# The clip of the projected rows of batch 1 moves from VectorE on PSUM to GpSimd on SBUF

## The chip, the cores and the metric

The kernel runs on one core of a Trainium2 chip. The time is the device time of one execution in microseconds. Before the change the median of three runs is 1516.16 us (1514.95 to 1519.41).

A core has five engines that matter here, each with a queue of its own that it works through in order: TensorE (PE in the profile), VectorE (DVE), ScalarE (ACT), GpSimd (POOL) and SyncE (SP), which only issues DMAs. GpSimd issues DMAs from its queue too. Engines wait for each other by semaphores. Matmuls write to PSUM, which has eight banks; SBUF holds everything else that is on the chip.

## The reference, cut to what matters

One transformer block whose attention and linear layer work beside each other on the same normalised input; B = 2, S = 1024, D = 1024, 32 heads of 32 channels, all in float32.

```python
xn  = layernorm(x)
qkv = clip(xn @ Wqkv.T, -8, 8)              # clip on all of q, k and v
q, k, v = split(qkv)
q = layer_norm(q, q_ln_w, q_ln_b)           # over all 1024 channels
k = layer_norm(k, k_ln_w, k_ln_b)
scores = q @ k.T * 32**-0.5 + slope[h] * (kpos - qpos), causal
attn = softmax(scores) @ v @ Wout.T
out = x + attn + (xn @ binarized(weight).T + bias)
```

The clip at 8 stands between the projections and the normalisation of q and k, and ahead of the use of v.

## The kernel before

**Projections.** Tokens go in pairs of 128-token tiles; batch b has four pairs. For one pair and one of k, q, v, the product with a 1024x1024 weight is made as a 2x2 block product with seven products in place of eight (`seven`, line 622). Each of the seven takes four matmuls of 128x512 into one PSUM bank, in the order 11, 21, t2, t3, t4, t1, 22. `combine` (line 643) adds the products up: `take` (line 672) is called after each of the seven; product 11 goes to SBUF by ScalarE, t2, t3 and t1 become running sums `u` and `u3` in SBUF by one VectorE operation each (`plus`, `less`), and the four halves of the two finished rows come out in `whole` (line 664): row a gets its first half from product 21 and its second from 22, row b from t4 and t1. `whole` first adds the running sum to the bank in place, on VectorE, and then clips the bank into the row (`kraw`, `qraw` or `vraw`, 128x1024), again on VectorE. For the output projection `bound` is None, and one add writes the row.

**What follows a row.** When row b is whole (after t1) and when row a is (after 22), `ready` is called. For k and q, `to_channels` (line 835) is put among the side jobs: statistics of both halves on VectorE (`stats_of`, line 703; BATCH_NORM_STATS2 in the profile), their aggregate, the reciprocal root on ScalarE (`spread`, line 709), a few short VectorE operations, the normalisation in place on ScalarE, transposes in 32x32 blocks on VectorE, and DMAs to DRAM from GpSimd's queue. For v, GpSimd's queue issues the DMA of the row at once.

**Attention.** A block is one batch, 512 query rows and a group of four heads; there are 32. `first_scores` (line 1276) makes scores for a unit of rows in four banks and takes their maximum on VectorE (CUSTOM_DVE on `s`, with `rel`; the read of `mx` follows); after that these banks are free. `shifts` (line 1313) turns the maxima into bf16 rows: five short GpSimd operations on `sh` and `shift_b`, then, one step later, a transpose `trs` on TensorE. `second_scores` (line 1337) makes transposed scores in four banks, less the shift, adds the causal mask on VectorE (`behind`), and ScalarE's exponential writes `pT`. `add_up_parts` (line 1411) sums the `pT` tiles of a block on GpSimd; the sum is the denominator that `divide` (line 1446) reads with the matmuls `den`. `weigh_values` multiplies `pT` with the values.

**Order.** Nothing is rescheduled: each engine executes its instructions in the order in which the program issues them. Batch 0's projections stand first (0 to some 320 us). The loop over steps (line 1520) then issues, per step, one unit of first scores, the shifts of a closed block, the denominators, the weighing, one unit of second scores, and then `fill` (line 1166), which issues a share of the remaining products one after the other: batch 1's k, q and v projections during batch 0's attention, then the binary linear layer and the output projection during batch 1's. After each two products' pieces `fill` advances the side jobs. So a projection's VectorE and GpSimd operations stand between those of two steps of attention.

**Banks.** Seven of the eight PSUM banks are shared by scores and products. `score_bank` (line 565) picks, at build time, the bank that has been idle longest by a model of the engines' times (`Clocks`, line 83 for the durations of one instruction); the eighth holds the weighed values. A matmul into a bank waits until its last reader is done. A row tile (`raw_tile`, line 556) has four buffers.

All operations of the kernel are recorded by one helper, so their line in the profile is L148, and they are told apart by their tiles: `mm_k` and `mm_k_t` are the products of k (t for those with a summed weight), `kraw` its rows; likewise q and v.

Of the kernel before, what the change touches and what calls it, by code (L numbers as in the profile page):

```python
# [12 lines left out]
ALU = mybir.AluOpType  # L13
# [21 lines left out]
class Clocks:  # L35
# [35 lines left out]
    def ready(self, eng, outs, ins):  # L71
        t = 0.0
        for ap, also_read in [(a, False) for a in ins] + [(a, True) for a in outs]:
            name = ap.tensor.name
            t = max(t, self.free.get(name, 0.0))
            p0, p1, lo, hi = self.spot(ap)
            for (q0, q1, l, h), (w, r, by) in self.log.get(name, {}).items():
                w = 0.0 if by == eng == "pe" else w
                if q0 < p1 and p0 < q1 and l < hi and lo < h:
                    t = max(t, w, r if also_read else 0.0)  # L80
        return t
# [112 lines left out]
def parallel_block_kernel(  # L194
# [37 lines left out]
    nc = Program(tc.nc, clocks)  # L232
# [170 lines left out]
    def half(n):  # L403
        return slice(n * HALF, (n + 1) * HALF)
# [154 lines left out]
    def half_tile(name):  # L559
        return work.tile([P, HALF], FP, tag="half", name=name, bufs=2)  # L560
# [82 lines left out]
    def combine(name, ra, rb, ready, rest=None, bound=None):  # L643


        h = {}

        def put(i, n):
            if rest:
                row = (ra, rb)[i][:, half(n)]  # L650
                if (i, n) != (0, 1):
                    nc.gpsimd.tensor_tensor(row, row, rest[i][:, half(n)], ALU.add)
                ready(i, row, n)

        def plus(dst, ps, other, op=ALU.add):
            nc.vector.tensor_tensor(dst, ps, other, op)

        def less(dst, ps, other):
            plus(dst, ps, other, ALU.subtract)

        def whole(i, n, ps, other, op=ALU.add):
            row = (ra, rb)[i][:, half(n)]
            if bound is None:
                plus(row, ps, other, op)
            else:
                plus(ps, ps, other, op)
                nc.vector.tensor_scalar(row, ps, -bound, bound, ALU.max, ALU.min)  # L670

        def take(block, ps):
            if block == "11":
                h["u"] = half_tile(f"u_{name}")
                nc.scalar.copy(h["u"], ps)
            elif block == "21":
                whole(0, 0, ps, h["u"])
                put(0, 0)
            elif block == "t2":
                plus(h["u"], ps, h["u"])  # L680
            elif block == "t3":
                h["u3"] = half_tile(f"u3_{name}")
                plus(h["u3"], ps, h["u"])
            elif block == "t4":
                whole(1, 0, ps, h["u3"])
                put(1, 0)
            elif block == "t1":
                less(h["u"], ps, h["u"])
                whole(1, 1, ps, h.pop("u3"), ALU.subtract)
                put(1, 1)  # L690
                if rest:
                    nc.gpsimd.tensor_tensor(h["u"], h["u"], rest[0][:, half(1)], ALU.add)
                else:
                    ready(1, rb)
            else:
                whole(0, 1, ps, h.pop("u"))
                put(0, 1)
                if not rest:
                    ready(0, ra)

        return take
# [719 lines left out]
    late = []  # L1421
# [187 lines left out]
```

## Time and profile before

| | |
|---|---|
| median of three runs | 1516.16 us (1514.95 to 1519.41) |
| profiled execution's own time | 1518.33 us |
| its span | 1516.5 us |
| mean granted TensorE clock | 0.994 |
| TensorE busy | 1473.9 us (97%) |
| VectorE busy | 967.2 us (64%) |
| GpSimd busy | 1045.4 us (69%) |
| ScalarE busy | 630.1 us (42%) |
| clip of a half row, VectorE, 128x512 | 0.692 us, 96 of them |
| add in place in a bank, VectorE, 128x512 | 0.695 us for mm_k |
| statistics of a half row, VectorE | 0.680 us |
| two-input add, GpSimd, 128x512 | 1.311 us |

How to read the profile's rows: times are microseconds, unless they are in a mean per instruction, which is in nanoseconds. A group's row gives engine, operation, written tile, an arrow and the tiles read, the shape and count, then busy time and mean, then the idle time just before these instructions and what ended it. A row of waits gives who waited, for whom, the sum, how many times, and the longest. A row of stretches gives the stretch and its length, then busy time and count of instructions of PE, PEld (weight loads), DVE, ACT and POOL, the granted clock, and the share and rate of the DMA engines. A row of the timeline gives the start, the duration from the first to the last of like instructions, the instruction, how many, and in brackets how long the engine had been idle and what ended that.

### The profile page before, as it was taken

How to read it: one execution, taken by the hardware profiler on the slowest of the kernel's cores; microseconds unless marked ns; L12 is line 12 of the kernel's file. 1: busy time of each engine (PE TensorE's matmuls, PEld its weight loads, DVE VectorE, ACT ScalarE, POOL GpSimd, SP SyncE). 2: the span in 40 equal slices, each digit the busy share in tenths (PEclk: the TensorE clock that was granted, in tenths of full speed). 3: DMA queues.
4: the chain of work that ended last, by engine and by line, in shares of the span. 5: the costliest groups of instructions: out<-in, count | busy, mean ns of one | idle time of the engine just before them, and what ended most of it. 6: DMA issues, size and time to landing. Idle time of an engine off the chain costs nothing.

```text
span 1516.5 us, 24240 instructions
## 1 busy us (share of the span) xinstructions
PE 1473.9 (97%) x8060; PEld 637.5 (42%) x8060; DVE 967.2 (64%) x2718; ACT 630.1 (42%) x1203; POOL 1045.4 (69%) x1336
## 2 busy tenths in 40 slices
PE   7999999999999999999999999999999999999998
PEld 3444444444434333333333344555655333333333
DVE  6866586868778776677556565666655666555322
ACT  3322132204556543544343573655554444443430
POOL 4587287333886678768747698767788778777661
PEclk9999999999999999999999998999999999999999
DMA  8889389682436764699335476667678213321232
GB/s 298 277 271 303 100 271 283 221 296 77 137 102 206 235 188 87 158 224 299 98 121 174 155 242 160 152 135 162 146 159 230 61 52 97 91 65 42 60 80 56
DMA packets 140909, 249.08 MB, mean 164 GB/s; under 512 B 12528, under 2 KB 69360, under 8 KB 138992
## 3 DMA queue, kind: packets, MB, share of 16 engines
q1 hardware_dynamic: 111392, 153.14, 31.1%
q0 software_dynamic: 29392, 94.39, 25.9%
q8 instruction: 64, 1.05, 0.3%
q14 instruction: 61, 0.50, 0.1%
HBM read 159.66 MB, written 107.74 MB: 176 GB/s over the span
## 4 chain that ended last, share of the span: by engine, by line
PE 82%; DVE 10%; issue 3%; POOL 2%; DMA 1%; ACT 1%; POOLq 0%; DVEq 0%; ACTq 0%; SPq 0%
PE s L148 20%; PE mm_f L148 8%; PE mm_o_t L148 7%; PE o L148 7%; PE mm_v_t L148 7%; PE mm_q_t L148 7%; PE mm_k_t L148 6%; PE mm_o L148 5%; PE mm_v L148 5%; PE mm_q L148 5%; DVE s L148 3%; PE mm_k L148 3%; PE den L148 2%; DMA x<-in_x_dram 1%; DVE mx L148 1%
## 5 line engine op out<-in xcount | busy, mean ns | idle before, releaser
L148 POOL TENSOR_TENSOR pT<-pT,pT 128x512 f32<-128x512 f32 (+3 forms) x628 | 579.5, 980 | 129.5 <-ACT pT L148 119.1
L148 ACT ACTIVATE pT<-s,kpos 128x512 f32<-128x512 f32 (+3 forms) x768 | 378.2, 590 | 441.0 <-DVE s L148 271.2
L148 DVE CUSTOM_DVE_ANT_0 s<-s,rel 128x512 f32<-128x512 f32 (+3 forms) x512 | 283.4, 600 | 54.4 <-PE s L148 47.9
L148 PE MATMUL s<-kg,qg 32*128 32x512 f32 (+3 forms) x1536 | 169.7, 523 | 1.4 <-DVE qraw L148 0.9
L148 PE MATMUL s<-qg,kg 32*128 32x512 f32 (+3 forms) x1536 | 164.6, 500 | 0.0
L148 PE MATMUL o<-pT,vg 128*32 128x512 f32 (+3 forms) x1536 | 157.7, 495 | 2.5 <-ACT pT L148 2.5
L148 DVE CUSTOM_DVE_ANT_0 s<-s,rel,mx 128x512 f32<-128x512 f32 (+3 forms) x256 | 140.9, 589 | 23.8 <-PE s L148 21.5
L148 PE MATMUL mm_f<-sg,hl 128*128 128x512 f32 x512 | 126.2, 399 | 2.1 <-DVE mx L148 2.1
L148 PE MATMUL mm_o_t<-w_o_t,ot 128*128 128x512 f32 x256 | 116.5, 601 | 0.0
L148 DVE TENSOR_TENSOR s<-s,behind 128x256 f32<-128x256 f32 (+1 forms) x320 | 98.7, 378 | 24.6 <-PE s L148 24.6
L148 PEld LDWEIGHTS s<-kg,qg 32*128 32x128 f32 x1536 | 66.6, 184 | 109.5 <-issue 71.7
L148 DVE DVE_READ_ACCUMULATOR2_ANT mx<- 128x1 f32 x768 | 109.1, 142 | 0.0
L148 PEld LDWEIGHTS mm_f<-sg,hl 128*128 128x128 f32 x512 | 93.9, 188 | 33.4 <-DVE mx L148 12.5
L148 PE MATMUL mm_v_t<-w_v_t,xp 128*128 128x512 f32 x224 | 101.7, 600 | 2.0 <-POOL w_v_t L148 1.6
L148 PE MATMUL mm_q_t<-w_q_t,xp 128*128 128x512 f32 x224 | 100.6, 598 | 0.0
L148 PE MATMUL s<-rows,minus_b 12*128 12x512 bf16 (+3 forms) x768 | 82.7, 329 | 14.1 <-DVE mx L148 13.3
L148 PEld LDWEIGHTS s<-qg,kg 32*128 32x128 f32 x1536 | 77.2, 185 | 29.3 <-issue 20.4
L148 PE MATMUL mm_v<-w_v,xp 128*128 128x512 f32 x192 | 88.6, 609 | 0.0
L148 PE MATMUL mm_o<-w_o,ot 128*128 128x512 f32 x192 | 87.8, 602 | 0.0
L148 PE MATMUL mm_q<-w_q,xp 128*128 128x512 f32 x192 | 86.3, 598 | 0.0
L148 PEld LDWEIGHTS o<-pT,vg 128*32 128x32 f32 x1536 | 39.2, 109 | 109.3 <-issue 90.2
L148 POOL TENSOR_TENSOR ot<-inv,ot 128x512 f32<-128x512 f32 x16 | 20.4, 1272 | 85.4 <-ACT inv L148 85.4
(201 smaller groups left out, 1863.3 us busy)
## 6 DMA issues: line engine op xcount, KB each, us to landing
xp<-xd SPq DMA_DIRECT2D x8, 1792.0 KB, 8.2
kg<-kd SPq DMA_DIRECT2D x48, 256.0 KB, 5.2
vg<-vd SPq DMA_DIRECT2D x48, 256.0 KB, 5.9
wd_ot<-in_wout_t_dram POOLq DMA_DIRECT2D x11, 1024.0 KB, 9.5
x<-in_x_dram SPq DMA_DIRECT2D x16, 512.0 KB, 5.8
qg<-qd SPq DMA_DIRECT2D x32, 256.0 KB, 6.3
vd<-vraw POOLq DMA_DIRECT2D x16, 512.0 KB, 6.5
out_dram<-in_x_dram SPq DMA_DIRECT2D x16, 512.0 KB, 7.7
```

The source lines that it names most:

```text
L148: result = real(*args, **kw)
```

## The change

For batch 1 (the second character of the name is the batch: `k1_0` is pair 0 of k of batch 1), the last add of a half row writes the row in SBUF, unclipped, and reads the bank only once; GpSimd then clips the half row in place in SBUF. For batch 0 the two VectorE operations stay as they are: an add in place in the bank, and the clip from the bank into the row.

```diff
             row = (ra, rb)[i][:, half(n)]
             if bound is None:
                 plus(row, ps, other, op)
-            else:
-                plus(ps, ps, other, op)
-                nc.vector.tensor_scalar(row, ps, -bound, bound, ALU.max, ALU.min)
+                return
+            late = name[1] != "0"
+            plus(row if late else ps, ps, other, op)
+            eng, src = (nc.gpsimd, row) if late else (nc.vector, ps)
+            eng.tensor_scalar(row, src, -bound, bound, ALU.max, ALU.min)
```

In the built program the order of the instructions on every engine is the same but for this: 48 clips are missing from VectorE's queue, and 48 stand in GpSimd's, each where the half row came out. The model that picks the banks sees the changed operations, so some score tiles and products lie in another bank than before.

## The prediction

> **What bounds the kernel now.** I read the page first: shares of busy time, slices, and the chain that ended last.
>
> ```profile
> span 1516.5 us, 24240 instructions
> PE 1473.9 (97%) x8060; PEld 637.5 (42%) x8060; DVE 967.2 (64%) x2718; ACT 630.1 (42%) x1203; POOL 1045.4 (69%) x1336
> PE 82%; DVE 10%; issue 3%; POOL 2%; DMA 1%; ACT 1%; POOLq 0%; DVEq 0%; ACTq 0%; SPq 0%
> ```
>
> TensorE is busy 97% of the span and carries 82% of the chain. VectorE has a tenth of the chain although it is 64% busy. So a shorter VectorE pays only where TensorE waits for it. Batch 1's projections stand between 320 and 910 us (first and last kraw to vraw clip of that batch: 331 and 902 us), so I asked for the busy time of three stretches there and for TensorE's waits between 320 and 910 us.
>
> ```profile
> 320.00:520.00 200.00, 193.52 (x1255) 80.06 (x1255) 156.97 (x475) 96.82 (x200) 126.97 (x189) 1.00 0.53 160
> 520.00:720.00 200.00, 194.33 (x1087) 73.93 (x1086) 142.71 (x403) 91.51 (x173) 153.94 (x176) 0.99 0.71 187
> 720.00:910.00 190.00, 184.91 (x1074) 72.96 (x1073) 111.86 (x323) 95.63 (x176) 136.31 (x158) 1.00 0.49 159
> PE s L148 <- DVE mx L148: 11.7, 32, 0.9
> PE mm_k_t L148 <- DVE mx L148: 1.3, 3, 0.4
> PE den L148 <- DVE vraw L148: 1.1, 1, 1.1
> PE trs L148 <- POOL shift_b L148: 0.5, 1, 0.5
> ```
>
> The columns of the first three are PE, PEld, DVE, ACT, POOL. TensorE idles 590.0 - 572.8 = 17.2 us, nearly all of it waiting for VectorE to free a score bank: many short waits, the longest 1.1 us. That is the ceiling of any gain. GpSimd is already 64, 77 and 72% busy, and it runs in order.
>
> **Prices.** From the groups of VectorE and GpSimd, shapes kept apart, and from the tiles rel and kpos:
>
> ```profile
> L148 DVE TENSOR_SCALAR kraw<-mm_k 128x512 f32<-128x512 f32 x16 | 11.1, 692 | 0.5
> L148 DVE TENSOR_TENSOR or<-mm_o,u_o 128x512 f32<-128x512 f32 x16 | 11.1, 692 | 44.3 <-PE mm_o L148 29.3 <-issue 10.8 <-POOL u_o L148 2.6
> L148 POOL TENSOR_TENSOR pT<-pT,pT 128x512 f32<-128x512 f32 x256 | 320.0, 1311 | 72.8 <-ACT pT L148 72.6
> L148 POOL TENSOR_SCALAR_AFFINE_SELECT rel<-rel x1: 1041/1041/1041, 2.3 to 2.3; 128x1024 f32<-128x1024 f32 x1
> L148 POOL TENSOR_SCALAR kpos<-off x32: 220/233/692, 11.9 to 40.3; 128x8 f32<-128x8 f32 x32
> ```
>
> **Part 1, the clip leaves VectorE.** 48 clips (three projections, four pairs of token tiles, four quarters) of 0.69 us: 33.2 us off VectorE. The add that remains costs the same into SBUF as in place: 0.692 us for or<-mm_o,u_o, which already reads PSUM and writes SBUF, against 0.695 us for mm_k<-mm_k,u_k. In the timeline I went through TensorE's 46 waits between 320 and 910 us. 29 of them follow a clip within 6 us with VectorE idle at most 0.15 us in between, so the clip itself made the score bank late there. Each recovers at most its own length or the clip's 0.69 us; together 10.2 us. The other 7 us follow a stretch in which VectorE had itself waited for TensorE, and stay. Bounds of the gain: 0 (every wait is replaced by the next bank's) and 10.2 us; I take all of it less what part 3 spoils, since these waits are shorter than the clip.
>
> **Part 2, GpSimd gets 48 clips.** No row shows a 128x512 one-input operation with two ALU steps on GpSimd. The nearest rows: the affine select of 1024 elements (1.04 us), and kpos with 8 elements (0.233 us median). The slope of the affine select is (1041 - 293)/896 = 0.835 ns an element (the 128x128 one on ident took 293 ns), so 512 elements make 0.61 us by that row and 0.233 + 504 x 0.835 ns = 0.65 us by kpos with that slope. Upper end: the two-input add, 1.31 us. I take 0.65 us, as the same operation is nearest, and keep 0.61 to 1.31. Load: 48 x 0.65 = 31 us on 417 us busy in 590, so 76%; it does not become the bound by load. The Trainium skill ("GPSIMD Engine Reference", section Engine selection) speaks against the change: elementwise work belongs on VectorE, GpSimd being about twice as slow for two inputs and roughly at line rate for one. By twice VectorE's 0.69 us a clip would be 1.38 us and the sum below about +4.4 us instead of -1.7; the slope of the affine select stands on the side of the one-input half of that rule. No run here yet shows the clip itself.
>
> What is queued behind a clip on GpSimd: where the row is written after GpSimd had got there, it waits for VectorE's add, and the shift chain behind it (sh, shift_b, read by the transpose trs on TensorE) starts late. That happens at 327, 343 and 369 us, by 4.9, 4.2 and 5.1 us. But trs follows one step later, at 341.7, 360.2 and 384.4 us, against shift_b at 328.3, 344.7 and 370.7: 9 to 15 us of slack. Cost 0. At 897.3 us the slack is 1.9 us (shift_b ends 895.35); two clips ahead of it and TensorE's own gain of 0.9 us in that stretch leave -0.3: cost 0.4 us. The last sums that the denominators read end 2 us or more before the den matmuls; one clip fits. The value rows' DMAs are issued by GpSimd behind the clip anyway, up to 2.5 us later, and are loaded much later: 0. SP issues nothing different.
>
> **Part 3, a new wait.** After product t1 of a pair (row b) and after product 22 (row a) VectorE's next step for a q or k row is its statistics (BATCH_NORM_STATS2 on both halves). They used to follow VectorE's own clip. Now they wait for GpSimd, which must first finish the probability sums queued ahead, and behind them on VectorE stand the next add and the score maxima that free TensorE's banks. The worst place:
>
> ```profile
> 402.85 8.24 POOL L148 TENSOR_TENSOR pT<-pT,pT 128x384 f32<-128x384 f32 x12
> 405.20 0.69 DVE L148 TENSOR_TENSOR mm_k_t<-mm_k_t,u_k 128x512 f32<-128x512 f32 x1
> 406.53 1.28 DVE L148 BATCH_NORM_STATS2 stats_k<-kraw 128x6 f32<-128x512 f32 x2
> 409.36 0.42 DVE L148 CUSTOM_DVE_ANT_0 s<-s,rel 128x256 f32<-128x256 f32 x1
> 410.53 0.37 PE L148 MATMUL s<-rows,minus_b 12*128 12x512 bf16 x1 [0.58 <-DVE mx L148]
> ```
>
> In the order of the built program the row's first clip stands after the eighth of the twelve sums, its second after the twelfth. The sums end at 411.1; with two clips the row is ready at 411.1 + 1.3 + 0.1 = 412.5 us, 6.0 us after the statistics began. The first maximum, which TensorE awaits at 410.5, comes 6.0 - 0.6 (the next row's clip, gone too) = 5.4 us later, and TensorE with it. I did the same ledger at all 16 such places, a delayed GpSimd instruction catching up in its own idle gaps. Row ready against old start of the statistics: k +2.2, -6.4, +6.0, -1.6, +0.5, -5.5, -4.5, +1.6; q -1.8, -2.1, +1.5, -2.1, -1.5, -3.5, -0.9, -2.9 us. Of the five late ones, that at 355 us reaches TensorE (2.2 - 0.6 = 1.6 us); those at 455, 513 and 601 us run into 0.8, 1.7 and 0.8 us in which VectorE waited for TensorE next, and into the missing clip: 0. Total 7.0 us. At those two places the waits counted as recovered (0.56 and 0.58 us) are lost as well.
>
> **Sum.** -10.2 + 1.1 (gain spoiled) + 7.0 + 0.4 = -1.7 us. At 1.31 us a clip the same ledger gives stalls of 2.9, 7.3, 2.4, 2.3 and 2.8 us with 11 us on TensorE, 1.7 us at trs and a gain of 8.4: +4 us. The profiled execution took 1518.33 us (span 1516.5), 2.2 us above the median of the three runs, 1516.16. From it: 1516.6; beside the median: 1514.5. I say 1515. What a measurement of this kernel can tell from no change is about 0.3%, 4.5 us.
>
> **The rivals.**
> - Net within 4.5 us (the forecast): relief and new waits cancel. Chance 0.42.
> - Faster: the statistics' waits are hidden. If TensorE has products to issue at 410 us or the planner's changed bank choice frees a score bank earlier, the 7.0 us shrink to 2 or less: -10.2 + 1.1 + 2 = -7, so 1509 us. Against it: TensorE's queue is in order and already waited 0.58 us for that bank. Chance 0.24.
> - Slower: the stalls go deeper because a clip costs 1.31 us and nothing absorbs them. The ledger's late rows (18.4 us with two small ones more) less the seven missing clips at 0.6 are 14 us, less a gain of 8.4: +5.7, so 1522 us. It decides from about 13 us of stall on TensorE. For it: a GpSimd that is 76% busy is late by 2 to 6 us at most of these rows already. Chance 0.2.
> - Slower: the relief is not collected, as each freed wait re-forms at the next bank. Then 7.4 us of loss stand against a quarter of the gain: +5, so 1521. Chance 0.12.
> - That nothing moves at all (the clip still on VectorE) the program's order excludes: 48 rows less on VectorE, 48 more on GpSimd. The remaining 0.02 is a mishap further up, 1530 or more.
>
> Faster 0.24, same 0.42, slower 0.34. The range: from the whole relief (-10, 1506) to the slower rivals with 5 us added where both meet (1527), leaving out a tenth on each side. The likeliest case alone: 1511.7 to 1520.
>
> **What the new profile should show.** GpSimd TENSOR_SCALAR on kraw, qraw, vraw, 16 each, near 0.65 us; VectorE 33 us less busy; stats_k waiting for POOL, about 6 us at 406 us and 2 us at 355; TensorE's waits on mx down to about half except there. I am wrong if stats_q waits add up too, if the clip is above 1.3 us, or if TensorE's idle time in the three stretches leaves 10 to 22 us.

## The result, and the profile after

The changed kernel takes 1532.09 us (median of four runs, 1530.63 to 1533.09) beside 1515.83 us for the kernel before in the same comparison: ratio 1.0102, 95% interval 1.0088 to 1.0116. It is slower by 16 us. The forecast was 1515 us, range 1506 to 1527. The profiled execution took 1530.63 us with a span of 1528.8 us, 12.3 us more than the profiled execution before; the traced execution before lies 2.5 us above the median of its kernel and the traced one after 1.5 us below the median of its own, so some 4 of the 16 us cannot be found by comparing these two traces.

The page of the changed kernel: span, busy time and the chain that ended last.

```profile
span 1528.8 us, 24185 instructions
PE 1475.5 (97%) x8060; PEld 637.8 (42%) x8060; DVE 935.7 (61%) x2670; ACT 629.8 (41%) x1203; POOL 1137.3 (74%) x1384
PE 76%; POOL 10%; DVE 6%; issue 4%; DMA 2%; ACT 2%; POOLq 0%; DVEq 0%; ACTq 0%; SPq 0%
```

VectorE is 31.5 us less busy, as the change intends. GpSimd is 91.9 us busier, three times what the forecast put there, and it has gone from 2% to 10% of the chain. TensorE is busy 1.6 us more and idle 10.7 us more (span less busy time: 53.3 us, 42.6 before), and its mean granted clock is 0.988 beside 0.994: the time is for the most part in its gaps.

The tile kraw of the changed kernel (duration in ns: least, median, greatest), then waits of VectorE at the statistics and of TensorE between 320 and 930 us, and last TensorE's wait for mx in that stretch before the change:

```profile
L148 POOL TENSOR_SCALAR kraw<-kraw x16: 1909/1914/1937, 331.4 to 526.9; 128x512 f32<-128x512 f32 x16
L148 DVE TENSOR_TENSOR kraw<-mm_k,u_k x8: 634/691/693, 330.6 to 521.0; 128x512 f32<-128x512 f32 x8
...
DVE stats_k L148 <- POOL kraw L148: 19.8, 6, 4.6
DVE stats_q L148 <- POOL qraw L148: 14.2, 9, 4.5
...
PE s L148 <- DVE kraw L148: 9.6, 3, 6.9
PE s L148 <- DVE mx L148: 9.3, 22, 1.5
PE trs L148 <- POOL shift_b L148: 3.2, 2, 2.0
PE s L148 <- DVE qraw L148: 3.1, 2, 2.2
...
PE s L148 <- DVE mx L148: 12.7, 34, 0.9
```

A clip of a half row costs 1.91 us on GpSimd, not 0.65. VectorE's remaining add costs 0.69 us into SBUF, as expected. VectorE stands 34.0 us at the statistics of k and q, waiting for clips; before, it stood there 0. TensorE's waits for mx fall from 12.7 to 9.3 us, but its waits on banks that the adds into kraw and qraw free are 12.7 us, where those rows' banks had cost 1.1, and those for the shift rows 3.2, where they had cost 0.5.

The place that the forecast picked as the worst, in the timeline of the changed kernel, GpSimd, VectorE, TensorE in turn, and then the ten microseconds from 415 us (the eighth column, 0.50, is the granted clock). The last two rows are the same score matmuls and the same ten microseconds in the kernel before:

```profile
405.56 5.49 POOL L148 TENSOR_TENSOR pT<-pT,pT 128x384 f32<-128x384 f32 x8
411.14 1.92 POOL L148 TENSOR_SCALAR kraw<-kraw 128x512 f32<-128x512 f32 x1
413.14 2.76 POOL L148 TENSOR_TENSOR pT<-pT,pT 128x256 f32<-128x256 f32 x4
415.99 1.91 POOL L148 TENSOR_SCALAR kraw<-kraw 128x512 f32<-128x512 f32 x1
...
413.09 0.69 DVE L148 BATCH_NORM_STATS2 stats_k<-kraw 128x6 f32<-128x512 f32 x1 [4.59 <-POOL kraw L148]
417.94 0.69 DVE L148 BATCH_NORM_STATS2 stats_k<-kraw 128x6 f32<-128x512 f32 x1 [4.15 <-POOL kraw L148]
418.79 0.64 DVE L148 TENSOR_TENSOR kraw<-mm_k,u_k 128x512 f32<-128x512 f32 x1
...
419.48 0.58 PE L148 MATMUL s<-rows,minus_b 12*128 12x512 bf16 x1 [6.90 <-DVE kraw L148]
420.40 2.29 PE L148 MATMUL s<-qg,kg 32*128 32x512 f32 x8
...
415.00:425.00 10.00, 5.18 (x13) 1.99 (x13) 6.72 (x28) 2.67 (x6) 5.78 (x9) 0.50 0.21 69
...
410.54 1.23 PE L148 MATMUL s<-qg,kg 32*128 32x512 f32 x8
415.00:425.00 10.00, 10.00 (x87) 4.13 (x90) 8.64 (x23) 8.34 (x18) 5.58 (x8) 1.00 0.34 101
```

VectorE waits 8.7 us in two pieces, TensorE 6.9 us behind it. The clock granted around this gap was 0.50, where the kernel before had 1.00 from 415 to 425 us, and the eight score matmuls took 2.29 us where they took 1.23 us before. I call lag how much later the same matmul starts than in the trace before; its times are those of the kernel before. It grows by 9.6 us here. Over the whole it stands at 0.3 us at 332 us, 2.1 at 372, 11.8 at 413, 13.5 at 473, 16.3 at 675, 9.2 at 857, 12.9 at 917, and 12.3 from 938 us to the end: k loses, q loses a little more, v regains, and v's last pair loses again.

### The profile page after: what moved, and what is told of

Read it like the earlier page. It is cut to its first block, busy times and chain, and to the rows that moved or that the text cites. A ratio compares the mean times of both kernels' runs of the same rounds, so it can differ in the third digit from the quotient of the medians.

```text
span 1528.8 us, 24185 instructions
## 1 busy us (share of the span) xinstructions
PE 1475.5 (97%) x8060; PEld 637.8 (42%) x8060; DVE 935.7 (61%) x2670; ACT 629.8 (41%) x1203; POOL 1137.3 (74%) x1384
## 3 DMA queue, kind: packets, MB, share of 16 engines
q8 instruction: 64, 1.05, 0.3%
## 4 chain that ended last, share of the span: by engine, by line
PE 76%; POOL 10%; DVE 6%; issue 4%; DMA 2%; ACT 2%; POOLq 0%; DVEq 0%; ACTq 0%; SPq 0%
PE s L148 19%; PE mm_f L148 7%; PE mm_o_t L148 7%; PE o L148 7%; PE mm_v_t L148 7%; PE mm_q_t L148 6%; PE mm_o L148 5%; PE mm_v L148 5%; PE mm_k_t L148 4%; PE mm_q L148 4%; POOL pT L148 4%; PE mm_k L148 3%; DVE s L148 2%; PE den L148 2%; DMA x<-in_x_dram 1%
## 5 line engine op out<-in xcount | busy, mean ns | idle before, releaser
L148 DVE CUSTOM_DVE_ANT_0 s<-s,rel,mx 128x512 f32<-128x512 f32 (+3 forms) x256 | 140.9, 589 | 27.4 <-PE s L148 25.2
L148 PE MATMUL mm_q<-w_q,xp 128*128 128x512 f32 x192 | 89.8, 618 | 0.0
L148 PEld LDWEIGHTS mm_o_t<-w_o_t,ot 128*128 128x128 f32 x256 | 46.7, 190 | 62.8 <-issue 52.3
```

The source lines that it names most:

```text
L148: result = real(*args, **kw)
```

## The experiments

Theory W: the loss is VectorE's wait at the statistics for a clip that stands deep in GpSimd's queue. Theory L: the loss is GpSimd's load, which makes sums, shift rows and DMAs late. Every edit is against the changed kernel unless the text says before.

**v alone.**

```diff
-            late = name[1] != "0"
+            late = name[1] != "0" and name[0] == "v"
```

> Only the 16 clips of batch 1's v go to GpSimd; k and q keep both VectorE operations. Theory W (the loss is VectorE's wait for the clip at the statistics of k and q): v has no statistics, so no loss; the 11 us of clips taken from VectorE free a few score banks earlier, 1511 to 1517 us. Theory L (the loss is GpSimd's load, which makes sums, shift rows and DMAs late): a third of the added GpSimd time stays, so about a third of the 16 us, 1519 to 1523 us.

Measured 1517.7 us beside 1516.9, ratio 1.0007 [0.9997, 1.0017]; the bracket, here and below, is the 95% interval. That is 0.7 us above the range of W and below that of L: a third of the load costs next to nothing, against L. But nor is anything gained. The lag against before falls to -3.5 us at 853 us, then rises to -0.5 us at 934 us; TensorE's waits for shift rows are 2.6 us in this run, 0.5 before.

**One ALU step.** The lower bound of the clip is left out.

```diff
-            eng.tensor_scalar(row, src, -bound, bound, ALU.max, ALU.min)
+            if late:
+                eng.tensor_scalar(row, src, bound, None, ALU.min)
+            else:
+                eng.tensor_scalar(row, src, -bound, bound, ALU.max, ALU.min)
```

> The changed kernel with only the upper bound applied on GpSimd (one ALU step in place of two; the lower bound is left out for batch 1). If the price of 1.91 us lies in the second step, the operation takes 0.6 to 1.0 us, and the forecast's own sum at such a price (+0 to +2 us) is put to the test: 1513 to 1519 us. If a one-step operation takes about as long, 1530 us, and the price is that of the operation as such. Theory L at half the load: 1522 to 1525 us.

Measured 1518.92 us, 1.0020 [1.0007, 1.0033]. The operation still takes 1.49 us (tile kraw of this run):

```profile
L148 POOL TENSOR_SCALAR kraw<-kraw x16: 1480/1486/1506, 331.5 to 524.5; 128x512 f32<-128x512 f32 x16
```

So most of the price is the operation, 0.43 us the second step; neither price that the expectation tied to its two cases came out. Yet 0.43 us less a clip takes 12 (by the ratios) to 14 (by the medians) of the 16 us away. In both built programs every PSUM tile lies in the same bank, so this is no matter of which banks were picked. VectorE's waits for GpSimd at the statistics, between 320 and 945 us of this run:

```profile
DVE stats_k L148 <- POOL kraw L148: 16.9, 6, 4.2
DVE stats_q L148 <- POOL qraw L148: 8.2, 8, 3.7
```

They are 25.1 us against 34.0. At k little changes: the lag still reaches 11.1 us at 451 us. At q's rows, most of which had 0.9 to 3.5 us to spare in the forecast's ledger, the lag then falls to 2.4 us at 732 us, where the changed kernel's ends at 12.7. Waits are only a part of this: TensorE's on banks of kraw and qraw and for the shift rows are 10.6 us here against 15.9. Of the 13.3 us between the two traces' spans, 7.0 are TensorE's busy time (1468.5 us, at a mean clock of 0.993 beside 0.988); which of the clock's changes follow from the waits is not shown.

**Statistics five turns later, with and without the clips on GpSimd.** The same edit on the changed kernel (late_stats) and on the kernel before (late_stats_before):

```diff
+        for _ in range(5 * b):
+            yield 0.0
         yield from spread(raw, stats_of(raw, name), name)
```

> The changed kernel, but the statistics of batch 1's k and q rows are issued five turns of the side jobs later (some 20 us), so that GpSimd's clip is long done; the clips stay on GpSimd at 1.91 us. Theory W: VectorE's waits of 34 us for kraw and qraw fall under 3 us, and 1514 to 1520 us (what remains are the late shift rows, 3 us). Theory L: GpSimd's load is the same, 1527 to 1532 us.

> The kernel before, with the statistics of batch 1's k and q rows issued five turns of the side jobs later, and no clip on GpSimd. It tells what the move of the side jobs itself cost in late_stats (1548.6 us). If the move is what cost: 1540 us or more, and the clips on GpSimd cost little once nothing waits for them. If the move is harmless: 1514 to 1520 us, and late_stats shows a loss by GpSimd's load of some 30 us (theory L).

Measured 1548.58 us, 1.0214 [1.0199, 1.0230] with the clips on GpSimd, and 1548.29 us, 1.0204 [1.0177, 1.0231] without. My expectation of late_stats missed because the move costs 32 us by itself. By the two traces it puts VectorE behind ScalarE's reciprocal root (11.7 us for q, 11.6 for k without the clips). The pair still tells something: with no wait for them at the statistics, 48 clips of 1.91 us on GpSimd leave the time unchanged. That is against L, if weakly, since the 32 us of other waits may hide a load.

**No wait, the same work.** The statistics read a constant tile of the same shape; those of the rows are left out.

```diff
-        yield from spread(raw, stats_of(raw, name), name)
+        yield from spread(raw, stats_of(raw, name, plain if b else None), name)
```

> The changed kernel, with the statistics of batch 1's k and q rows taken over a constant tile of the same shape (the true statistics are left out), so that VectorE does the same work at the same place and waits for no clip; GpSimd does all 48 clips at 1.91 us. Theory W (the wait at the statistics is the loss): VectorE's waits for GpSimd vanish, TensorE keeps what the missing VectorE clips give, 1509 to 1517 us. Theory L (GpSimd's load is the loss): 1525 to 1532 us. Waits of the shift rows on TensorE, 3 us, remain by both.

Measured 1510.47 us, 0.9960 [0.9945, 0.9975]. With all 48 clips on GpSimd and only the wait gone, the kernel is 6 us faster than before, some 22 us faster than the changed one (by their ratios). This settles W: the wait, with what follows from it, is the loss. Some PSUM tiles lie in other banks than in the changed kernel, which this run does not hold fixed. Waits of TensorE in this run, 320 to 945 us:

```profile
PE s L148 <- DVE mx L148: 7.8, 21, 0.9
PE trs L148 <- POOL shift_b L148: 3.2, 2, 2.1
```

No wait on kraw or qraw is left. TensorE is 11.7 us ahead of before at 857 us, and gives 3.8 us back up to 917 us, where the shift rows come late.

**k alone, q alone.** The edit of k_only; q_only has "q1" in its place:

```diff
-            late = name[1] != "0"
+            late = name[:2] == "k1"
```

> Only the 16 clips of batch 1's k go to GpSimd. By the changed kernel's shift against before (13 us gathered between 350 and 480 us, at three rows of statistics), theory W: 1524 to 1529 us. Theory L, a third of the load: 1519 to 1523 us.

> Only the 16 clips of batch 1's q go to GpSimd. The changed kernel gathered 2 to 3 us between 520 and 720 us, so theory W: 1516 to 1521 us. Theory L, a third of the load: 1519 to 1523 us.

Measured 1529.74 us, 1.0085 [1.0056, 1.0114] for k, and 1517.67 us, 1.0000 [0.9988, 1.0013] for q. The load is a third in each, the loss is nearly all k's (0.7 us above the range of W). k has the row at 413 us: its lag grows by 9.8 us there, with TensorE's gap of 6.9 us, as in the changed kernel. q's clips are waited for too, 13.6 us on VectorE in q_only, but there is relief to pay for it: in stats_elsewhere, with nothing waiting, TensorE gains 7.2 us among q's rows (473 to 732 us) and only 1.0 us among k's. The losses of k, q and v alone add up to some 14 us of the 16.

**The bank freed earlier, the clip on VectorE in SBUF.** An attempt to have the relief without GpSimd:

```diff
-            eng, src = (nc.gpsimd, row) if late else (nc.vector, ps)
+            eng, src = (nc.vector, row) if late else (nc.vector, ps)
```

> The add writes the row as in the changed kernel, but VectorE clips it in SBUF (batch 1 only), so that the bank is free after one operation and nothing new waits for GpSimd. If the clip takes 0.69 us there as from PSUM: score banks are no earlier, product banks 0.69 us earlier; 1513 to 1516 us. If it takes about half, VectorE is relieved of 16 us and TensorE's short waits after a clip fall by about half: 1508 to 1513 us. Theories W and L say nothing against either.

Measured 1554.13 us, 1.0254 [1.0238, 1.0269]: the worst of all, and against both cases of the expectation. The tile kraw and one place in the timeline of this run:

```profile
L148 DVE TENSOR_SCALAR kraw<-kraw x16: 426/428/5532, 332.1 to 522.8; 128x512 f32<-128x512 f32 x16
...
405.12 8.22 POOL L148 TENSOR_TENSOR pT<-pT,pT 128x384 f32<-128x384 f32 x12
...
408.10 5.53 DVE L148 TENSOR_SCALAR kraw<-kraw 128x512 f32<-128x512 f32 x1
413.55 1.27 DVE L148 BATCH_NORM_STATS2 stats_k<-kraw 128x6 f32<-128x512 f32 x2
```

From SBUF to SBUF the clip takes 0.43 us instead of 0.69. But one that meets a run of GpSimd's sums can last until that run ends: here 5.53 us, to 0.3 us past the end of twelve sums, and 1.7 to 4.9 us at nine other places. Elsewhere it came in behind the one sum that was running (1.05 us at 611 us), and the next sum then took 1.46 us, not 1.31. The 48 clips together are 56.4 us where PSUM as source would cost 33.2, and TensorE's waits for mx are 35.0 us in this run, 12.7 before. The Trainium skill ("Advanced Engine Details and Errata", VectorE Performance Modes) has the rule: VectorE's two-port modes, which need source and destination in SBUF, and GpSimd's instructions share a port and block each other. The run agrees, and shows that VectorE can wait for a whole run of back-to-back GpSimd instructions, as in the 5.53 us above.

**v without its last pair.**

```diff
-            late = name[1] != "0"
+            late = name[:2] == "v1" and name != "v1_3"
```

> GpSimd clips v's first three pairs of batch 1 only (12 clips); k, q and v's last pair stay on VectorE. In the run with all of v TensorE was 3.5 us ahead at 853 us and lost 3 us at the last pair, where GpSimd's queue is full and the shift rows came late. If that is the reason, the 3.5 us stay: 1512 to 1514.5 us (ratio 0.9975). If the loss after 853 us has another cause (banks picked otherwise): 1516 to 1518 us.

Measured 1509.75 us, 0.9967 [0.9954, 0.9980], beside 1515.14 us, 2 us below the expected range. The 3.5 us stay (lag -3.5 us at 917 us). Between 917 and 938 us the lag goes on to -7.3 us, and in these two traces that is the clock: the profiled execution before had 0.50 from 920 to 930 us and this one 1.00. It does not explain all of the distance between the medians: where the mean granted clock was 0.999, the kernel before took 1514.5 us (median of seven executions) and this one 1509.6 (of five), so some 1.4 us of gain beyond the lag stay open. The two stretches, before and v_early; the eighth column is the clock:

```profile
920.00:930.00 10.00, 9.79 (x39) 3.55 (x40) 4.83 (x20) 1.52 (x3) 6.16 (x6) 0.50 0.70 157
```

```profile
920.00:930.00 10.00, 8.88 (x50) 4.27 (x46) 6.84 (x23) 3.45 (x6) 8.74 (x9) 1.00 0.28 54
```

Why the clock was granted there in one and not in the other stays open.

**First quarters of k and q with it.** mix_21 adds product 21's quarter; its edit follows. first_halves adds t4's as well, with `n == 0` in place of `(i, n) == (0, 0)`:

```diff
-            late = name[1] != "0"
+            late = name[1] != "0" and ((i, n) == (0, 0) if name[0] != "v" else name != "v1_3")
```

> As the run before this one, and the first quarter (product 21) of each q and k row pair of batch 1 is clipped on GpSimd too: 8 clips whose statistics come only after product 22, some 25 us later. Theory W: nobody waits for these, and the missing VectorE clips free banks: 1511 to 1514 us. Theory L: 20 clips more on GpSimd, 1518 to 1522 us.

> As the run before this one, and the t4 quarter of k and q goes to GpSimd too: 8 clips more, with 4 to 9 us between VectorE's add and the statistics. Theory W: where GpSimd lags by 11 us (the k row at 406 us) VectorE waits about 4 us and TensorE with it, elsewhere little: 1514 to 1518 us.

Measured 1509.49 us, 0.9958 [0.9942, 0.9975] and 1512.92 us, 0.9982 [0.9971, 0.9993]. They are 1.5 and 1.1 us below their ranges. Clips that nobody waits for cost nothing; mix_21 cannot be told from v_early. The t4 quarters bring the wait at the k row back (3.9 us of VectorE, 3.4 of TensorE at 414 us), and the lag grows by some 7 us there.

**Two turns later, and the control.** As the edit with five turns, with two; late_two_before is the same edit on the kernel before, late_two_v3 leaves v's last pair on VectorE besides.

> The changed kernel, all 48 clips on GpSimd, statistics two turns of the side jobs later instead of five. If the move's own cost grows with the turns (32 us at five), some 12 us, and the waits at the statistics are gone for the most part: 1520 to 1528 us. If the cost comes only from a certain place that two turns do not reach: 1511 to 1516 us. If the waits stay as without the move: 1530 us and more.

> The kernel before, no clip on GpSimd, statistics of batch 1's k and q two turns later: the control for late_two (1515.8 us). If the recovery in late_two is the wait that is gone, the move itself gains nothing: 1514 to 1520 us, and the 48 clips moved with nobody waiting gain 0 to 4 us. If the move itself gains 5 us or more (1511 or less), late_two still holds a loss by the clips.

> As late_two, but v's last pair stays on VectorE, so that no clip stands ahead of the shift rows at 890 us. In late_two TensorE was 6.6 us ahead at 857 us and lost 3.8 us up to 917 us. If these clips are why, the gain stays: 1507 to 1512 us. If not: 1514 to 1517 us.

Measured 1515.82 us, 0.9996 [0.9984, 1.0008]; 1515.26 us, 1.0000 [0.9989, 1.0012]; and 1509.47 us, 0.9957 [0.9940, 0.9973]. The move of two turns is free by itself; with it VectorE's waits for GpSimd at the statistics fall from 34.0 to 1.5 us (one left), and all 16 us are back. The last pair of v, two of whose clips stand ahead of the shift rows, is the cost that is left: in late_two the lag goes from -6.6 us at 857 us to -2.9 at 917, in late_two_v3 from -6.5 to -6.3 us. late_two_v3, mix_21 and v_early beat the kernel before by 0.3 to 0.4% and cannot be told from each other.

## Why the prediction was wrong, point by point

- **Part 1, the relief: right in size.** 10.2 us was forecast, at the waits that follow a clip. With nobody waiting for GpSimd, TensorE was 11.7 us ahead at 857 us (stats_elsewhere); in late_two it was 10.1 us ahead of late_two_before there.
- **Part 2, the price: this is the term that failed.** Forecast 0.65 us, between 0.61 and 1.31; measured 1.91. The step that failed is the slope: I took the nanoseconds an element of an affine select (0.835) for a TENSOR_SCALAR, whose only row before had 8 elements and so told its start-up alone. With kpos at 0.233 us for 8 elements, the 512 elements make 2.5 ns an element with one step and 3.3 with two. The upper end failed as well: a two-input add (1.31 us) was no bound, the one-input operation is dearer. The Trainium skill's rule that I weighed ("GPSIMD Engine Reference", Engine selection) said the right thing by its advice and the wrong one by its reason: one-input operations at line rate is not what this operation showed, neither with one step (1.49 us) nor with two. Why the operation is so dear no run shows. The kernel's own planner makes the same mistake: `Clocks` prices the clip on GpSimd at 0.15 + 0.001 x 512 = 0.66 us, so the banks were picked for a clip of a third of the real length. What a right price there would bring is not tested.
- **Part 3, the new wait: right in place and kind, too small in size.** With 1.91 us put into the same ledger, VectorE's waits at the 16 places sum to about 34 us; the trace has 34.0 (19.8 for k, 14.2 for q). So close a sum is partly luck: at single places the ledger is off by 2 to 3 us. At 406 us the ledger gives 8.5 us, the trace 8.7. With 0.65 us it had given 12 us.
- **From waits to TensorE: too linear.** The ledger's sum rises by some 8 us per microsecond of price, so 1.91 us would have given about +9 us; measured +16 (+12 between the profiled executions). Two things lie between. VectorE's delay at q's rows uses up their slack: at 1.49 us a clip TensorE makes up 8.7 us of lag between 451 and 732 us, at 1.91 us it makes up none. And a long gap cost more than its length: at 413 us 9.6 us of lag for about 7 us of gap, with a clock of 0.50 around it, which the forecast did not count.
- **The shift rows: right place, wrong size.** 0.4 us was forecast at 897 us (the slack that was worked out, -0.3 us, makes it 0.3). With two clips of 1.91 us ahead of it TensorE lost 3 to 4 us there (late_two against late_two_v3).
- **Which rival.** The outcome is the first slower rival, a dearer clip and deeper stalls, given 0.2 and priced at 1522 us: right in kind, 10 us short. Its point of decision, about 13 us of stall on TensorE, was reached (12.7 us on the banks of kraw and qraw, and 3.2 for the shift rows). All three signs of being wrong came out: stats_q waits 14.2 us, the clip is above 1.3 us, and TensorE is idle 27.4 us in the three stretches, not 10 to 22. The second slower rival, that freed waits re-form, is refuted by stats_elsewhere.

## What to carry to other kernels

In this kernel, work that was moved to a slower queue cost little by its load, but for the shift rows behind it; it cost by the first instruction that waited for its result on an engine whose next steps others need. So look for that reader and issue it later, or move only the parts that are read late. And take the price of an operation from a row of that same operation at a similar size: a short row of it tells the start-up only, and the slope of a different operation is not a bound.

## What the runs showed of the hardware that I had not expected

- GpSimd's TENSOR_SCALAR on 128x512 float32 in place took 1.91 us with two ALU steps and 1.49 us with one, more than its two-input add of the same size (1.31 us).
- VectorE's clip took 0.69 us from PSUM, 0.43 us from SBUF to SBUF, and up to 5.53 us from SBUF to SBUF while GpSimd ran sums back to back, until these ended.
- Around a gap of 6.9 us on TensorE the clock granted was 0.50 over ten microseconds; eight score matmuls that took 1.23 us before took 2.29 us.
